# A third tile of each l fetched row by row, its DMAs issued from ScalarE in groups of eight

## The chip, the core and the metric

The kernel runs on one core of a Trainium2 chip. The metric is the device time of one execution in microseconds (us). The engines are named as in the profile: PE (TensorE), DVE (VectorE), ACT (ScalarE), POOL (GpSimd) and SP (SyncE). An l is one of the 200 positions of the history, and a step is one eighth of an l.

## The reference

A recommendation model scores 16384 users (B). Each has 200 items of history (L). For every l and user a row of 64 floats is looked up in a table of items, and an attention net of 36 hidden units weighs it:

```python
u = u_emb[user]; it = i_emb[item]; c = c_emb[cate]
h = i_emb[hist]                                   # L x B x 64
itb = broadcast(it, h.shape)
feat = concatenate([h, itb, h - itb, h * itb], axis=-1)
a = dice(feat @ au_W1 + au_b1, au_alpha, axis=1)  # statistics over B, for each l
w = a @ au_W2 + au_b2
cur = sum(w * h, axis=0)                          # over l
z = concatenate([u, it, c, cur], axis=-1)
z = dice(z @ W1 + b1, alpha1, axis=0)
z = dice(z @ W2 + b2, alpha2, axis=0)
return z @ W3 + b3
```

`dice(x)` normalises x by its mean and variance along the axis, takes a sigmoid p of that, and returns x * (p + alpha * (1 - p)). The lookup `i_emb[hist]` is 3,276,800 rows of 256 bytes.

## The kernel before, in words

The 16384 users of one l are 128 tiles (NT) of 128 users, one user a partition. Sixteen tiles (TD) make a chunk c, eight chunks (ND) an l, and the kernel takes one chunk a step: step k belongs to l = k // 8 and c = k % 8. A loop (L406, turned four times) holds 45 l each, written out; the last 20 l and the head come after it.

There are two ways in which a tile's rows get into the chip's memory.

- By gather: `fetch` (L270) issues one indirect DMA per tile on POOL (L117). It takes 128 row numbers from a column of `idx` and brings 128 rows. All tiles but two of each l come so: 126.
- By address: the last tile of the chunks c = 3 and c = 7 (`SIDES`, L26) is fetched row by row on SP. `rows_by_address` (L254) loads sixteen addresses from `addr` into registers at once (L258, TENSOR_LOAD) and issues sixteen DMAs of one row each (L265: a MOVE and a DMA). They land in one of three `side` tiles. In the turn of that chunk ACT copies the side tile into the chunk's rows (L301). `ask` (L356) spreads this over SP: half an l, four steps, for a tile.

The chunk's rows lie in one of five row buffers (`ROWS`). Step k, in the program's order:

1. `fetch(k)`: POOL issues the chunk's gathers, 16, or 15 where a side tile belongs to the chunk.
2. `gate(k - 10)` on ACT (L278, L279), `weights(k - 10)`: a product on DVE (L282) and a matmul into `wb`.
3. `hidden(k - 2)`: ACT brings the hidden layer from `px` (L290); `measure(k - 2)`: DVE takes its statistics (L295).
4. `turn(k - 1)`: the copy of the side tile (L301, two chunks of eight), four transposes on DVE (L146) into hT, matmuls on hT and on the item's rows, and a copy of hT into `ph` on ACT (L304).
5. `weigh(k - 10)` on DVE (L286, L287) adds to the sum over l; `product(k - 1)`: DVE (L307) and a last matmul into `px`.
6. Once per l, `moments`: small DVE operations and a square root on ACT (L160).

Each engine works through its own instructions in that order, which is written out by hand (`tc.manual_schedule`); semaphores put in by the framework hold an engine where it needs another's result. A DMA that SP issues by the framework waits for the DMA eight before it, since eight semaphores go round; so does a gather on POOL.

Per l SP also loads the row numbers of the next l (c = 0, L130) and its addresses (c = 2, L135), which DVE scales to bytes at c = 4 (L138). `column` (L87) says which column of `idx` a tile has.

Of the kernel before, what the change touches and what calls it, by code (L numbers as in the profile page):

```python
# [9 lines left out]
I32 = mybir.dt.int32  # L10
# [4 lines left out]
P = 128  # L15
D = 64
# [5 lines left out]
ROWS = 5  # L22
LAG = 10
XR = 9
IDX = 3
SIDES = (3, 7)  # L26
LOAD = 16
ROW = 4 * D
U8 = mybir.dt.uint8

# [2 lines left out]
def din_kernel(  # L33
# [24 lines left out]
    nc = tc.nc  # L58
    L, B = r_hist.shape
    NT = B // P  # L60
    TD = 2 * CD // P
    ND = NT // TD
    V = i_emb.shape[0]
# [2 lines left out]
    ZA = P // 2  # L66
    ZB = Z1 - ZA
    NS = len(SIDES)
    NC = NT - NS
    BODY = L - L % LPB if L > LPB else 0  # L70
    STATS = nc.vector.BN_STATS_DIM
# [5 lines left out]
    def make(name, *shape, dt=F32):  # L77
        return const.tile(list(shape), dt, name=name)

    def col(v):  # L80
        return v.rearrange("(p o) -> p o", o=1)
# [5 lines left out]
    def column(c, n):  # L87
        if c in SIDES and n == TD - 1:
            return NC + SIDES.index(c)
        return c * TD + n - sum(s < c for s in SIDES)  # L90

    def columns(v):
        return v[: NC * P].rearrange("(p n) -> p n", n=NC)

# [5 lines left out]
    rows = [make(f"rows{i}", P, TD, D) for i in range(ROWS)]  # L100
    hT = [make(f"hT{i}", P, CD) for i in range(LAG)]
    xs = [make(f"xs{i}", P, CD) for i in range(XR)]
    itT = [make(f"itT{c}", P, CD) for c in range(ND)]
    curT = [make(f"curT{c}", P, CD) for c in range(ND)]
    hm = make("hm", P, CD)
    y = make("y", P, CD)
    ucT = [make(f"ucT{i}", P, CD) for i in range(4)]
    idx = [make(f"idx{i}", P, NC, dt=I32) for i in range(IDX)]
    ids = [make(f"ids{i}", P, NT, dt=I32) for i in range(3)]
    side = [make(f"side{i}", P, D) for i in range(3)]  # L110
    addr = [make(f"addr{i}", 1, NS * P, dt=I32) for i in range(3)]
    stats = [make(f"st{i}", P, 2 * ND, STATS) for i in range(3)]
    rstds = [make(f"rs{i}", P, 1) for i in range(3)]
# [2 lines left out]
    def gather(dst, ids, n, table):  # L116
        nc.gpsimd.indirect_dma_start(  # L117
            out=dst[:, n, :],
            out_offset=None,
            in_=table,  # L120
            in_offset=bass.IndirectOffsetOnAxis(ap=ids, axis=0),
        )

    def load_ids(t, v):
        nc.sync.dma_start(t[:, :NC], columns(v))
        for s in range(NS):
            nc.sync.dma_start(t[:, NC + s : NC + s + 1], col(v[(NC + s) * P : (NC + s + 1) * P]))

    def load_hist_ids(i, l):
        nc.sync.dma_start(  # L130
            idx[i], r_hist[ds(l, 1), : NC * P].rearrange("l (p n) -> p (l n)", n=NC)
        )

    def load_addresses(i, l):
        nc.sync.dma_start(addr[i], r_hist[ds(l, 1), NC * P :])  # L135

    def scale_addresses(i):
        nc.vector.tensor_scalar_mul(addr[i], addr[i], ROW)  # L138

# [3 lines left out]
    def transpose(dst, of):  # L143
        for i in range(2):
            for e in range(2):
                nc.vector.transpose(by_tile(dst[ts(e, D)], i), of[ts(i, D), :, ts(e, S)])  # L146

    def layer(dst, pairs, first=True, last=True):
        for i in range(2):
            for j, (lhsT, rhs) in enumerate(pairs):  # L150
                nc.tensor.matmul(  # L151
                    dst[:, ts(i, CH)], lhsT, rhs[:, ts(i, CH)],
                    start=(first and j == 0), stop=(last and j == len(pairs) - 1),
                    skip_group_check=not (first and last),
                )
# [59 lines left out]
    al1a, al1b, al12 = make("al1a", P, 1), make("al1b", P, 1), make("al12", P, 1)  # L215
    same_a = make("same_a", P, P)
    same_b = make("same_b", P, P)
    lanes = make("lanes", P, P, dt=I32)
    lane = make("lane", P, P, dt=I32)

    def head_weights():
        for t in (w1a, w1b, w2a, w2b, w3, bias2, al2):
# [28 lines left out]

    flat = i_emb.rearrange("v d -> (v d)").bitcast(U8)

    def rows_by_address(m, l, part, n):  # L254
        s, dst = m % NS, side[m % 3].bitcast(U8)
        for b in range(0, n, LOAD):
            p0 = part * n + b
            _, at = nc.values_load_multi_w_load_instructions(  # L258
                addr[l % 3][:, s * P + p0 : s * P + p0 + LOAD],
                engines=(mybir.EngineType.SP,), min_val=0, max_val=ROW * (V - 1),  # L260
                skip_runtime_bounds_check_because="the DMA checks the address against the table",
            )
            for j, a in enumerate(at):
                p = p0 + j
                nc.sync.dma_start(dst[p : p + 1], flat[ds(a, ROW)].rearrange("(o d) -> o d", o=1))  # L265

    def has_side(k):
        return k % ND in SIDES

    def fetch(k):  # L270
        l, c = divmod(k, ND)
        for n in range(TD - has_side(k)):
            j = column(c, n)
            gather(rows[k % ROWS], idx[l % IDX][:, j : j + 1], n, i_emb)

    def gate(k):
        i = k // ND % 3
        nc.scalar.activation(pg, xs[k % XR], AF.Sigmoid, bias=shifts[i], scale=rstds[i])  # L278
        nc.scalar.activation(pg, pg, AF.Identity, bias=au_al, scale=au_1al)  # L279

    def weights(k):
        nc.vector.tensor_mul(y, pg, xs[k % XR])  # L282
        layer(wb, [(blk_w, y)])

    def weigh(k):
        nc.vector.scalar_tensor_tensor(wb, wb, au_bias2, hT[k % LAG], ALU.add, ALU.mult)  # L286
        nc.vector.tensor_add(curT[k % ND], wb, curT[k % ND])  # L287

    def hidden(k):
        nc.scalar.activation(xs[k % XR], px, AF.Identity, bias=au_bias)  # L290

    def measure(k):
        l, c = divmod(k, ND)
        for i in range(2):
            nc.vector.bn_stats(stats[l % 3][:, 2 * c + i, :], xs[k % XR][:, ts(i, CH)])  # L295

    def turn(k):
        if has_side(k):
            l, c = divmod(k, ND)
            m = l * NS + SIDES.index(c)  # L300
            nc.scalar.copy(rows[k % ROWS][:, TD - 1], side[m % 3])  # L301
        transpose(hT[k % LAG], rows[k % ROWS])
        layer(px, [(blk_h, hT[k % LAG]), (blk_i, itT[k % ND])], last=False)
        nc.scalar.copy(ph, hT[k % LAG])  # L304

    def product(k):
        nc.vector.tensor_mul(hm, ph, itT[k % ND])  # L307
        layer(px, [(blk_m, hm)], first=False)
# [21 lines left out]
    def step(k, last=None):  # L330

        def has(j):
            return last is None or j <= last

        if has(k):
            fetch(k)
        if has(k - LAG):
            gate(k - LAG)
            weights(k - LAG)
        if has(k - 2):  # L340
            hidden(k - 2)
            measure(k - 2)
        if has(k - 1):
            turn(k - 1)
        if has(k - LAG):
            weigh(k - LAG)
        if has(k - 1):
            product(k - 1)
        if has(k - 2) and (k - 2) % ND == ND - 1:
            moments((k - 2) // ND)  # L350

    PER = ND // NS

    def ask(k, end):  # L356
        m, part = divmod(k + 1, PER)
        if m < end * NS:
            rows_by_address(m, m // NS, part, P // PER)

    def steps(l0, n, end):
        for k in range(n * ND):
# [10 lines left out]
    with tc.manual_schedule():  # L373
        load_ids(ids[0], r_item)
        load_hist_ids(0, 0)
        load_addresses(0, 0)
        load_ids(ids[1], r_cate)
        load_ids(ids[2], r_user)
        nc.gpsimd.iota(lanes, pattern=[[1, P]], base=P, channel_multiplier=-1)
        attention_weights()  # L380
        for t in (*hT, *xs, *side, hm):
            nc.vector.memset(t, 0.0)  # L382
        for t in curT:
            nc.vector.memset(t, 0.0)
        for i in range(3):
            nc.vector.memset(rstds[i], 0.0)
            nc.vector.memset(shifts[i], 0.0)  # L387
        nc.vector.bn_stats(stats[-1 % 3][:, 0, :], hm[:, :CH])
        for c in range(1, 2 * ND):
            nc.vector.tensor_copy(stats[-1 % 3][:, c, :], stats[-1 % 3][:, 0, :])  # L390
        scale_addresses(0)
        layer(px, [(blk_m, hm)])

        for c in range(ND + 1):
            if c < ND:
                for n in range(TD):
                    j = column(c, n)
                    gather(rows[c % ROWS], ids[0][:, j : j + 1], n, i_emb)
            if c:
                transpose(itT[c - 1], rows[(c - 1) % ROWS])  # L400
        nc.vector.memset(rows[-1 % ROWS], 0.0)
        ask(-1, L)
        head_weights()

# [35 lines left out]
    with tc.manual_schedule():  # L440
# [54 lines left out]
        for c in range(ND):  # L495
# [13 lines left out]
            for q in range(4):  # L509
                c = 4 * g + q  # L510
                n, j = TD - (c in SIDES), column(c, 0)
                of = res[g][ts(q, S)]
# [4 lines left out]
                if c in SIDES:  # L517
                    j = column(c, TD - 1)
# [33 lines left out]
```

## Time and profile before

| | |
|---|---|
| median of three runs | 32128.78 us (32128.46 to 32131.62) |
| the profiled execution | 32101.94 us |
| its span, first to last instruction | 32100.2 us |
| granted clock of TensorE in it, mean | 0.719 |
| busy share of PE, DVE, ACT, POOL | 49%, 46%, 24%, 75% |
| gathers on POOL | 25200 of history, 128 each of items, users and categories |
| rows by address on SP | 51200 DMAs of 256 bytes |
| moved by the DMA engines | 881.57 MB, 27 GB/s over the span |

How to read it: "busy" counts what the engine itself executes. Register moves, semaphores, register loads (TENSOR_LOAD) and the issuing of a DMA are the sequencer's and are not in it, so SP has no busy time at all, and ACT's share would not grow by DMAs that it issues. Idle time in front of a group of instructions is put down to what ended it; "issue" means that nothing in the profile ended it. In a group's line stand the engine, the operation, out<-in, the count, then busy us and mean ns of one, then idle us and what ended most of it. In a line of a window stand its ends, its length, the busy time with the count, the granted clock, the DMA engines' busy share and GB/s. A line of the timeline has the start, the duration, the engine, the line and the operation, the count, and in brackets the idle time before it and who ended it.

### The profile page before, as it was taken

The page shows a single profiled execution, that of the slowest core. Times are in us where ns is not written, and L with a number is a line of the kernel's source. Part 1 is how long each engine was busy: PE and PEld are TensorE (multiplying, and loading weights), DVE is VectorE, ACT ScalarE, POOL GpSimd, SP SyncE. Part 2 cuts the span into 40 slices and gives each one's busy share as a digit, 9 for nine tenths or more (in the row PEclk, how much of TensorE's full clock was granted, in tenths as well). Part 3 has the DMA queues.
Part 4 walks back from the last instruction along what each step waited for, and adds up shares of the span by engine and source line. Part 5 has one row for each costly group of instructions (what it writes and reads, how often), then busy time and mean ns, then how long its engine had stood idle before and what let it go on. Part 6 is the DMA issues. An engine that isn't in the chain of part 4 may idle for free. (4 is left out here: it accounts for less than half of the span.)

```text
span 32100.2 us, 224464 instructions
## 1 busy us (share of the span) xinstructions
PE 15661.4 (49%) x26020; PEld 6253.8 (19%) x26020; DVE 14921.9 (46%) x18956; ACT 7823.3 (24%) x7481; POOL 24139.4 (75%) x25589
## 2 busy tenths in 40 slices
PE   4444444444444444444445444454444444445445
PEld 1111121111111111111112111121111211112111
DVE  4444444444444444444444444444444444444443
ACT  2222222222222222222222222222222222222222
POOL 7777777777777777777777777777777777777776
PEclk7777767776777777777777777777777777777777
DMA  1111111111111111111111111111111111111111
GB/s 28 28 28 28 28 28 28 28 27 28 28 28 28 28 28 28 28 27 28 28 28 28 28 28 28 28 28 28 28 28 28 28 28 28 28 28 28 28 28 22
DMA packets 958596, 881.57 MB, mean 27 GB/s; under 512 B 547488, under 2 KB 547688, under 8 KB 957032
## 3 DMA queue, kind: packets, MB, share of 16 engines
q0 software_dynamic: 818688, 839.97, 11.8%
q1 hardware_dynamic: 138056, 27.05, 0.4%
q14 instruction: 1352, 11.08, 0.1%
q8 instruction: 212, 3.47, 0.0%
q10 hardware_dynamic: 288, 0.00, 0.0%
HBM read 865.03 MB, written 0.13 MB: 27 GB/s over the span
## 5 line engine op out<-in xcount | busy, mean ns | idle before, releaser
L117 POOL DMA_INDIRECT rows<-in_L_rec_i_emb,idx x25200 | 23776.6, 944 | 7706.1 <-issue 7132.8
L151 PE MATMUL px<-hT,blk_h 128*128 128x512 f32 x6404 | 5661.5, 983 | 15033.9 <-DVE hT L146 15033.9
L146 DVE STREAM_TRANSPOSE hT<-rows 64x512 f32<-64x512 f32 x6404 | 4519.1, 706 | 12085.3 <-DMA rows<-in_L_rec_i_emb,idx 11421.6
L304 ACT COPY ph<-hT 128x1024 f32<-128x1024 f32 x1601 | 1627.1, 1016 | 18738.7 <-DVE hT L146 18738.7
L151 PEld LDWEIGHTS px<-hT,blk_h 128*128 128x128 f32 x6404 | 1816.6, 314 | 18047.2 <-issue 17233.6
L151 PE MATMUL px<-itT,blk_i 128*128 128x512 f32 x6404 | 4735.4, 832 | 0.0
L151 PE MATMUL wb<-y,blk_w 128*128 128x512 f32 x6440 | 3413.4, 657 | 1245.9 <-DVE y L282 1230.2
L295 DVE BATCH_NORM_STATS2 st<-xs 128x6 f32<-128x512 f32 x3204 | 2058.3, 684 | 3704.4 <-ACT xs L290 3704.4
L151 PE MATMUL px<-hm,blk_m 128*128 128x512 f32 x6408 | 3036.9, 596 | 38.1 <-DVE hm L382 36.4
L290 ACT ACTIVATE xs<-px,au_bias 128x1024 f32<-128x1024 f32 x1602 | 1781.6, 1112 | 4164.1 <-PE px L151 4164.1
L151 PEld LDWEIGHTS px<-itT,blk_i 128*128 128x128 f32 x6404 | 1862.1, 291 | 2859.9 <-issue 2859.9
L282 DVE TENSOR_TENSOR y<-pg,xs 128x1024 f32<-128x1024 f32 x1610 | 1954.9, 1214 | 736.6 <-ACT pg L279 736.4
L286 DVE SCALAR_TENSOR_TENSOR wb<-wb,au_bias,hT 128x1024 f32<-128x1024 f32 x1610 | 2081.1, 1293 | 82.2 <-PE wb L151 30.0
L287 DVE TENSOR_TENSOR curT<-wb,curT 128x1024 f32<-128x1024 f32 x1610 | 1971.2, 1224 | 54.8
L278 ACT ACTIVATE pg<-xs,sh,rs 128x1024 f32<-128x1024 f32 x1610 | 1937.3, 1203 | 79.9 <-DVE sh L387 42.7
L307 DVE TENSOR_TENSOR hm<-ph,itT 128x1024 f32<-128x1024 f32 x1601 | 1942.5, 1213 | 0.0
L279 ACT ACTIVATE pg<-pg,au_al,au_1al 128x1024 f32<-128x1024 f32 x1610 | 1895.1, 1177 | 54.1
L151 PEld LDWEIGHTS wb<-y,blk_w 128*128 128x128 f32 x6440 | 1307.8, 207 | 2976.1 <-issue 1538.0
L151 PEld LDWEIGHTS px<-hm,blk_m 128*128 128x128 f32 x6408 | 1195.9, 191 | 1686.8 <-issue 1236.5
L278 ACT ACT_TABLE_LOAD x206 | 264.3, 1283 | 77.5 <-PEq L406 57.4
L160 ACT ACT_TABLE_LOAD x203 | 260.4, 1283 | 7.5 <-PE pg L461 4.0
L160 ACT ACTIVATE std<-var,eps 128x1 f32<-128x1 f32 x201 | 59.2, 294 | 710.6 <-DVE var L327 710.6
(147 smaller groups left out, 1531.7 us busy)
## 6 DMA issues: line engine op xcount, KB each, us to landing
side<-in_L_rec_i_emb SPq DMA_DIRECT2D x51200, 0.2 KB
rows<-in_L_rec_i_emb,idx POOLq DMA_INDIRECT x25200, 2.4
idx<-in_r_hist SPq DMA_DIRECT2D x200, 63.0 KB
addr<-in_r_hist SPq DMA_DIRECT2D x200, 1.0 KB
rows<-in_L_rec_i_emb,ids POOLq DMA_INDIRECT x128, 2.4
rows<-in_L_rec_c_emb,ids POOLq DMA_INDIRECT x128, 2.3
rows<-in_L_rec_u_emb,ids POOLq DMA_INDIRECT x128, 2.4
w1a<-in_L_rec_W SPq DMA_DIRECT2D x4, 32.0 KB
```

The lines of the kernel that those rows point to most:

```text
L117: nc.gpsimd.indirect_dma_start(out=dst[:, n, :], out_offset=None, in_=table, in_offset=bass.IndirectOffsetOnAxis(ap=ids, axis=0),)
L146: nc.vector.transpose(by_tile(dst[ts(e, D)], i), of[ts(i, D), :, ts(e, S)])
L151: nc.tensor.matmul(dst[:, ts(i, CH)], lhsT, rhs[:, ts(i, CH)], start=(first and j == 0), stop=(last and j == len(pairs) - 1), skip_group_c ...
L278: nc.scalar.activation(pg, xs[k % XR], AF.Sigmoid, bias=shifts[i], scale=rstds[i])
L279: nc.scalar.activation(pg, pg, AF.Identity, bias=au_al, scale=au_1al)
L282: nc.vector.tensor_mul(y, pg, xs[k % XR])
L286: nc.vector.scalar_tensor_tensor(wb, wb, au_bias2, hT[k % LAG], ALU.add, ALU.mult)
L287: nc.vector.tensor_add(curT[k % ND], wb, curT[k % ND])
L290: nc.scalar.activation(xs[k % XR], px, AF.Identity, bias=au_bias)
L295: nc.vector.bn_stats(stats[l % 3][:, 2 * c + i, :], xs[k % XR][:, ts(i, CH)])
L304: nc.scalar.copy(ph, hT[k % LAG])
L307: nc.vector.tensor_mul(hm, ph, itT[k % ND])
```

## The change

A third tile of each l, the last one of the chunk c = 6, is fetched row by row, and its 128 DMAs are issued by ACT. `SIDES` has three chunks, so 125 tiles of an l are gathered (NC = 125); SP keeps c = 3 and c = 7 as they were.

ACT's share is cut into sixteen groups of eight rows: one TENSOR_LOAD of eight addresses and eight DMAs. `scalar_rows` deals them over the steps c = 0 to 6 of the same l: two groups a step, three in the steps of c = 3 and c = 6, none in that of c = 7. A step's groups go alternately into two places of its program: after `gate` and `weights` (slot 0), and after `measure` (slot 1). With three groups, two are in slot 0.

The rows land in one of three new tiles, `aside`. Each has a semaphore of its own, `landed`, that all 128 DMAs raise by 16; the framework's semaphores are not used for these DMAs, so none of them waits for an earlier one. In the turn of c = 6 (in step c = 7) ACT waits for 16 * 128 on the semaphore, clears it, and copies the tile into the chunk's rows.

Two constant tiles, `lanes` and `lane`, share memory with `ucT` now, the address tile has 384 words and not 256, and the lists of row numbers at the start come in one more DMA each. The diff, cut to its core:

```diff
-SIDES = (3, 7)
+BY_SP = (3, 7)
+BY_ACT = 6
+SIDES = (3, 6, 7)
 LOAD = 16
+GROUP = 8
...
+    NB = len(BY_SP)
     NC = NT - NS
...
+    aside = [make(f"aside{i}", P, D) for i in range(3)]
+    landed = [tc.alloc_semaphore(f"landed{i}") for i in range(3)]
     addr = [make(f"addr{i}", 1, NS * P, dt=I32) for i in range(3)]
...
-    lanes = make("lanes", P, P, dt=I32)
-    lane = make("lane", P, P, dt=I32)
+    lanes, lane = (ucT[i][:, :P].bitcast(I32) for i in range(2))
...
+    def addresses(l, s, p0, n, engine):
+        _, at = nc.values_load_multi_w_load_instructions(
+            addr[l % 3][:, s * P + p0 : s * P + p0 + n],
+            engines=(engine,), min_val=0, max_val=ROW * (V - 1),
...
+        )
+        return [flat[ds(a, ROW)].rearrange("(o d) -> o d", o=1) for a in at]
+
+    def rows_by_sync(m, part, n):
+        l, j = divmod(m, NB)
+        s, dst = SIDES.index(BY_SP[j]), side[m % 3].bitcast(U8)
+        for p0 in range(part * n, part * n + n, LOAD):
+            for j, row in enumerate(addresses(l, s, p0, LOAD, mybir.EngineType.SP)):
+                nc.sync.dma_start(dst[p0 + j : p0 + j + 1], row)
...
+    def rows_by_scalar(l, part):
+        s, dst = SIDES.index(BY_ACT), aside[l % 3].bitcast(U8)
+        key = open_group.setdefault(l, f"rows{next(groups)}")
+        for j, row in enumerate(addresses(l, s, part * GROUP, GROUP, mybir.EngineType.Activation)):
+            p = part * GROUP + j
+            dma = nc.scalar.dma_start(dst[p : p + 1], row).then_inc(landed[l % 3], 16)
+            tc.no_tile_sem_insts.add(dma.ins.name)
+            tc.add_to_no_dep_group(key, dma.ins)
+
+    def take_rows_by_scalar(l):
+        fence = nc.scalar.wait_ge(landed[l % 3], 16 * P)
+        tc.declare_fence(fence.ins, group=open_group.pop(l))
+        nc.scalar.sem_clear(landed[l % 3])
+        return aside[l % 3]
...
     def turn(k):
         if has_side(k):
             l, c = divmod(k, ND)
-            m = l * NS + SIDES.index(c)
-            nc.scalar.copy(rows[k % ROWS][:, TD - 1], side[m % 3])
+            if c == BY_ACT and l >= 0:
+                of = take_rows_by_scalar(l)
...
+            else:
+                of = side[(l * NB + BY_SP.index(c)) % 3]
+            nc.scalar.copy(rows[k % ROWS][:, TD - 1], of)
...
             gate(k - LAG)
             weights(k - LAG)
+        if has(k):
+            scalar_rows(k, 0)
         if has(k - 2):
             hidden(k - 2)
             measure(k - 2)
+        if has(k):
+            scalar_rows(k, 1)
         if has(k - 1):
             turn(k - 1)
...
+    def scalar_rows(k, slot):
+        l, c = divmod(k, ND)
+        if c > BY_ACT:
+            return
+        n = P // GROUP
+        mine = range(c * n // (BY_ACT + 1), (c + 1) * n // (BY_ACT + 1))
+        for part in mine[slot::2]:
+            rows_by_scalar(l, part)
```

More of the change, by code (lines that the diff above doesn't have):

```diff
@@ L252, in din_kernel @@
     flat = i_emb.rearrange("v d -> (v d)").bitcast(U8)
[L254 to L265, printed above, removed]
+    def addresses(l, s, p0, n, engine):
+        _, at = nc.values_load_multi_w_load_instructions(
+            addr[l % 3][:, s * P + p0 : s * P + p0 + n],
+            engines=(engine,), min_val=0, max_val=ROW * (V - 1),
+            skip_runtime_bounds_check_because="the DMA checks the address against the table",
+        )
[6 more added lines that the diff above has]
+                nc.sync.dma_start(dst[p0 + j : p0 + j + 1], row)
+    groups = iter(range(10**6))
+    open_group = {}
+    def rows_by_scalar(l, part):
[11 more added lines that the diff above has]
+        return aside[l % 3]
     def has_side(k):
@@ L299, in turn @@
             l, c = divmod(k, ND)
-            m = l * NS + SIDES.index(c)
-            nc.scalar.copy(rows[k % ROWS][:, TD - 1], side[m % 3])
+            if c == BY_ACT and l >= 0:
+                of = take_rows_by_scalar(l)
+            elif c == BY_ACT:
+                of = aside[l % 3]
+            else:
+                of = side[(l * NB + BY_SP.index(c)) % 3]
+            nc.scalar.copy(rows[k % ROWS][:, TD - 1], of)
         transpose(hT[k % LAG], rows[k % ROWS])
@@ L350, in step @@
             moments((k - 2) // ND)
-    PER = ND // NS
+    PER = ND // NB
     def ask(k, end):
         m, part = divmod(k + 1, PER)
-        if m < end * NS:
-            rows_by_address(m, m // NS, part, P // PER)
+        if m < end * NB:
+            rows_by_sync(m, part, P // PER)
+    def scalar_rows(k, slot):
[6 more added lines that the diff above has]
+            rows_by_scalar(l, part)
     def steps(l0, n, end):
@@ L380, in din_kernel @@
         attention_weights()
-        for t in (*hT, *xs, *side, hm):
+        for t in (*hT, *xs, *side, *aside, hm):
             nc.vector.memset(t, 0.0)
```

## The prediction

> **What bounds the kernel now.** I read first the page's busy times and slices, then the group of gathers (L117), then that line in four long windows, to get a rate from the trace and not from a mean.
>
> ```profile
> PE 15661.4 (49%) x26020; PEld 6253.8 (19%) x26020; DVE 14921.9 (46%) x18956; ACT 7823.3 (24%) x7481; POOL 24139.4 (75%) x25589
> ...
> POOL 7777777777777777777777777777777777777776
> ...
> DMA  1111111111111111111111111111111111111111
> ...
> q0 software_dynamic: 818688, 839.97, 11.8%
> q1 hardware_dynamic: 138056, 27.05, 0.4%
> ...
> L117 POOL DMA_INDIRECT rows<-in_L_rec_i_emb,idx x25200 | 23776.6, 944 | 7706.1 <-issue 7132.8
> ```
>
> No engine is above 75%, but POOL is level in all forty slices, and 7132.8 of its 7706.1 us of idle time end with "issue": nothing that the profile shows is waited for. 944 ns of work and a gap after it that belongs to the instruction make one gather. The windows (length, busy, count) give the sum of the two:
>
> ```profile
> 2000.00:6000.00 4000.00, 3023.06 (x3205) 0.72 0.12 28
> 10000.00:14000.00 4000.00, 3023.05 (x3205) 0.72 0.12 28
> ```
>
> 4000 us hold 3205 gathers (one of them cut by an edge), twice the same: 4000 / 3204 = 1.2484 us. The whole run is that rate: first gather at 2.9 us, last at 31963.8, 25584 of them (25200 of history, 3 x 128 others), so 25583 distances. Four of them are longer, where the loop of L406 turns or ends (8.94, 7.15, 7.15 and 4.04 us, 27.3 in all); the other 25579 take 31933.6 us, 1.2484 each. After the last gather's start the head needs 136.4 us. 2.9 + 31933.6 + 27.3 + 136.4 = 32100.2, the span. So POOL's count of gathers sets the time, and nothing else does between 2.9 and 31963.8 us. One l is 126 gathers, 157.3 us.
>
> Everybody else waits for it. ACT's longest wait (18738.7 us) is for the transposes (hT, L146), and these wait for gathers to land (11421.6 us).
>
> **What is removed.** One gather per l: 125 in place of 126. 200 x 1.2484 = 249.7 us of POOL's own path, with no cover to fill it: the next gather moves up. On the profiled execution: span 32100.2 - 249.7 = 31850.5; its own time is 1.7 us above its span (32101.94), so 31852.2. The median of the three runs is 32128.78, 26.8 above the profiled execution; I keep that distance and take 32128.78 - 249.7 = 31879.
>
> **What is added on ACT.** Per l sixteen groups: a TENSOR_LOAD of eight addresses, eight pairs of MOVE and DMA. 200 x 128 = 25600 DMAs, 3200 loads. ACT has issued only two DMAs so far; SP issues this very DMA 51200 times, so SP's rows are the nearest:
>
> ```profile
> 15032.13 11.53 SPq L265 DMA_DIRECT2D side<-in_L_rec_i_emb  x32
> ```
> ```profile
> L258 SPq TENSOR_LOAD <-addr x3200: 1130/1229/1483, 47.1 to 31498.1; - x189
> ```
> ```profile
> L519 ACTq DMA_DIRECT2D out<-res x2: 373/396/418, 32078.5 to 32092.8; - x2
> ```
>
> 32 DMAs with one load among them take 11.53 us from the first one's start to the last one's end. (11.53 - 0.23 for the last DMA - 1.29 for the load and the gap after it) / 31 = 0.323 us a DMA, MOVE included. A group is then 1.23 + 8 x 0.32 = 3.79 us. From below: eight registers, not sixteen, are loaded; the Trainium skill (DMA: Bandwidth & Descriptors, Latency and other measured facts) gives about 0.6 us as a floor of that load, so an estimate of 0.6 + 2.56 = 3.2. From above: the longest load, 1.48, and DMAs as long as ACT's own longest, 0.418 plus 0.1 for the MOVE: 1.48 + 8 x 0.52 = 5.6. I take 3.79, since form and count are SP's. ACT's work in one l is 38.7 us (the window 15000 to 15157.4); one more copy of a side tile (L301, 0.234) makes 38.9; 38.9 + 16 x 3.79 = 99.6 us of a new l of 156.05. With 5.6: 128.5. ACT becomes the bound at (156.05 - 38.9) / 16 = 7.3 us a group, 0.76 us a DMA.
>
> **Where in a step it stands.** Averages do not show order, so here is one step on ACT, and two instructions of DVE after it.
>
> ```profile
> 15007.01 1.02 ACT L304 COPY ph<-hT 128x1024 f32<-128x1024 f32 x1 [9.04 <-DVE hT L146]
> 15007.96 1.20 ACT L278 ACTIVATE pg<-xs,sh,rs 128x1024 f32<-128x1024 f32 x1
> 15009.20 1.18 ACT L279 ACTIVATE pg<-pg,au_al,au_1al 128x1024 f32<-128x1024 f32 x1
> 15012.77 1.11 ACT L290 ACTIVATE xs<-px,au_bias 128x1024 f32<-128x1024 f32 x1 [2.39 <-PE px L151]
> 15026.90 1.02 ACT L304 COPY ph<-hT 128x1024 f32<-128x1024 f32 x1 [13.02 <-DVE hT L146]
> ```
> ```profile
> 15013.91 1.28 DVE L295 BATCH_NORM_STATS2 st<-xs 128x6 f32<-128x512 f32 x2 [2.09 <-ACT xs L290]
> 15023.98 2.88 DVE L146 STREAM_TRANSPOSE hT<-rows 64x512 f32<-64x512 f32 x4 [8.78 <-DMA rows<-in_L_rec_i_emb,idx]
> ```
>
> The first groups of a step come after L279 (ends 15010.38) and before L290; the others after L290 and before the next L304. Queued behind the first is L290, and behind that DVE's statistics, which stand before the next transposes in DVE's order; behind the second are the copies of a turn. With one group each: L290 ends at 15010.38 + 3.79 + 1.11 = 15015.3, statistics at 15016.6, second group at 15019.1. The worst steps (c = 3 and 6) have two groups first and one after: L290 ends at 15019.1, statistics at 15020.4, the last group at 15022.9. The transposes cannot start before 15023.98, since their gathers have not landed, and L304 not before 15026.90: 3.6 and 4.0 us are left, and the whole addition is hidden by POOL. With 5.6 us a group L290 ends at 15022.7 and the statistics at 15024.0, just on the edge. If that cover is gone, a step runs late, and then five row buffers cover: POOL needs the buffer of step k again 4 steps (some 78 us) after its last gather, and DVE frees it 2.4 + 2.9 us after. POOL waits only for a delay of over 70 us that is not made good, and the steps with fewer groups, c = 7 with none, make it good.
>
> **The added wait.** In the turn of c = 6 ACT waits for 2048 on a landed semaphore. Behind it stand the copy into the rows, the transposes and L304. The last group was issued a step before (nearly 20 us); a gather lands 2.2 to 4.3 us after its issue. Cost 0; from above one landing, 4.3 us a step, inside the row buffers, so also 0 on the end. No gain is possible from it.
>
> **SP, DVE, POOL, start and end.** SP keeps its two tiles: per l 16 x 1.23 + 256 x 0.32 = 102 us plus two index loads; it now idles
>
> ```profile
> SPq L258 <- DVE y L282: 10009.2, 195, 77.5
> ```
>
> some 51 us per l, which covers the longer address load (384 words). If both issuers share one generator, ACT's 128 x 0.32 = 41 us are taken from that idle time: 106 + 41 = 147 of 156, still hidden. DVE gets three memsets of 0.11 us and a longer L138 (0.28 us, once per l). Does a gather slow down when more of these DMAs run beside it? SP's stream comes and goes, so the trace answers: distances of gathers with none of SP's DMAs in them average 1.2483 us (9586 of them), with four 1.2486 (8755). At that slope the new DMAs cost at most 0.0003 x 25384 = 8 us if each gather met four more; ACT issues for 16 x 3.79 = 61 of 156 us, so some 3; from below 0. The three more id loads at the start are SP's. Prologue, loop turns and head stay: 0, with a few us either way. Sum: -249.7 + 0 to 10.
>
> **A rule that speaks against it.** The row first: sixteen DMA engines are 12% busy and the gather has a fixed rate. The Trainium skill (DMA: Bandwidth & Descriptors, Issuing engines are not separate DMA queues) says that DMAs started by several engines run on the same sixteen DMA engines and that spreading them saves only issue time, usually small. By the rule alone the change would be worth about 0, 32129. By the row issue time is the whole path, and its share is 200 x 1.2484. I go by the row.
>
> **Rivals.**
> 1. POOL's path shortened as summed: 31879, with the unknowns 31865 to 31900. Chance 0.84.
> 2. ACT's groups cost 5 to 7 us (an issue on ACT next to activations is dearer than on SP), steps run late by turns, and POOL loses part: half the gain, 32004. Against it: the 70 us of row buffers. Chance 0.05 above 0.2%.
> 3. The work is moved but the end does not follow: another chain, of DVE or SP, is as long as POOL's. SP with a shared generator comes nearest, 147 of 156; at 157 the time would be 32129. Chance 0.04.
> 4. Slower: ACT pays each row's round trip before it issues the next. The skill gives 0.8 us as the least round trip to memory (same page and section as the load's floor). A group is 1.23 + 8 x 0.8 = 7.63, ACT's l 38.9 + 122.1 = 161.0 against 157.3 now: 200 x 3.7 = +740, 32870. It decides from 0.76 us a DMA (slower than before from 0.77). Against it: SP's 0.32 for the same DMA, and the new semaphores hold nothing back until the turn. No row shows 128 in flight on one semaphore. Chance 0.07.
>
> **Numbers.** About 0.2% (64 us) is what a measurement of this kernel can tell from no change. Faster is cases 1 and 2: 0.89; within 0.2%: 0.04; slower: 0.07. The range takes case 1 with its unknowns, a few us between executions, and the near part of case 2: 31862 to 31935.
>
> **What would show it.** Right: 25000 gathers of history, 1.2484 us apart in the same windows; span near 31850; ACT's wait for hT shorter, SP's wait still tens of us per l; DMAs of ACT 0.32 us apart. Wrong: longer idle time at L117 ended by ACT or DVE (cases 2, 4), gathers over 1.259 us apart (249.7 / 25000 = 0.010 us eats it all), or transposes that wait for ACT and not for gathers.

## The result and the profile after

| | before | changed |
|---|---|---|
| median of four runs | 32129.93 us | 31890.28 us (31864.21 to 31894.12) |
| ratio to before, 95% interval | | 0.9924, [0.9906, 0.9941] |
| the profiled execution, its span | 32101.94, 32100.2 us | 31864.21, 31862.4 us |

The kernel became 0.76% faster. The forecast was 31879 for the median and 31850.5 for the span of the profiled execution; both are 11 to 12 us short. The changed kernel's four runs include the profiled one, which is 26 to 30 us under the other three; the profiled execution of the kernel before, not among its four, is as far under those. Where that distance comes from was not traced (at the end).

The page of the changed kernel: busy times, the gathers (L123 now), the new queue of ACT's DMAs.

```profile
PE 15641.2 (49%) x26020; PEld 6235.8 (20%) x26020; DVE 14956.3 (47%) x18959; ACT 7911.4 (25%) x7681; POOL 23951.3 (75%) x25389
...
q10 hardware_dynamic: 51632, 6.66, 0.1%
...
L123 POOL DMA_INDIRECT rows<-in_L_rec_i_emb,idx x25000 | 23588.4, 944 | 7656.7 <-issue 7249.9
```

POOL has 200 gathers fewer, of the same 944 ns, and still idles for nothing that the profile can name. ACT's busy time grew by 88 us only, 47 of them the 200 new copies, since issuing is not counted. The same windows as before, for the gathers alone:

```profile
2000.00:6000.00 4000.00, 3022.83 (x3205) 0.72 0.13 28
10000.00:14000.00 4000.00, 3022.66 (x3205) 0.72 0.13 28
```

3205 again: POOL's pace did not change, there is less of it. What ACT's sequencer spends is seen in the lines that load and issue (minimum, median and maximum in ns), and one step on ACT shows where it went:

```profile
L260 ACTq TENSOR_LOAD <-addr x3200: 709/723/1039, 48.6 to 31363.9; - x189
```
```profile
L283 ACTq DMA_DIRECT2D aside<-in_L_rec_i_emb x25600: 217/218/595, 49.4 to 31367.2; - x199
```
```profile
15008.46 1.02 ACT L335 COPY ph<-hT 128x1024 f32<-128x1024 f32 x1 [8.20 <-DVE hT L152]
15009.41 1.20 ACT L304 ACTIVATE pg<-xs,sh,rs 128x1024 f32<-128x1024 f32 x1
15010.65 1.18 ACT L305 ACTIVATE pg<-pg,au_al,au_1al 128x1024 f32<-128x1024 f32 x1
15011.50 2.61 ACTq L283 DMA_DIRECT2D aside<-in_L_rec_i_emb  x8
15014.22 1.11 ACT L316 ACTIVATE xs<-px,au_bias 128x1024 f32<-128x1024 f32 x1 [2.39 <-PE px L157]
15015.09 2.65 ACTq L283 DMA_DIRECT2D aside<-in_L_rec_i_emb  x8
15028.39 1.02 ACT L335 COPY ph<-hT 128x1024 f32<-128x1024 f32 x1 [13.06 <-DVE hT L152]
```

ACT's sequencer loads the addresses and starts to issue while the activation before still runs: in the trace the load starts at 15010.65 with L305, the first group's DMAs start at 15011.50, and L305 ends at 15011.83. The group ends at 15014.11, where ACT would have waited for PE anyway: L316 starts 2.39 us after L305's end, as L290 did after L279's in the kernel before. From the load's start to the last DMA's end this group takes 3.46 us; over all 3200 groups the median is 3.53. A DMA with its MOVE takes 0.31, the first of a group 0.55.

### The profile page after: what moved, and what is told of

Its sections match the earlier page's. It is cut to its first block, busy times and chain, and to the rows that moved or that the text cites. A ratio compares the mean times of both kernels' runs of the same rounds, so it can differ in the third digit from the quotient of the medians.

```text
span 31862.4 us, 279674 instructions
## 1 busy us (share of the span) xinstructions
PE 15641.2 (49%) x26020; PEld 6235.8 (20%) x26020; DVE 14956.3 (47%) x18959; ACT 7911.4 (25%) x7681; POOL 23951.3 (75%) x25389
## 5 line engine op out<-in xcount | busy, mean ns | idle before, releaser
L123 POOL DMA_INDIRECT rows<-in_L_rec_i_emb,idx x25000 | 23588.4, 944 | 7656.7 <-issue 7249.9
L335 ACT COPY ph<-hT 128x1024 f32<-128x1024 f32 x1601 | 1627.3, 1016 | 15569.4 <-DVE hT L152 15560.5
L316 ACT ACTIVATE xs<-px,au_bias 128x1024 f32<-128x1024 f32 x1602 | 1783.5, 1113 | 5882.8 <-PE px L157 2957.5
L308 DVE TENSOR_TENSOR y<-pg,xs 128x1024 f32<-128x1024 f32 x1610 | 1954.1, 1214 | 745.0 <-ACT pg L305 744.8
L305 ACT ACTIVATE pg<-pg,au_al,au_1al 128x1024 f32<-128x1024 f32 x1610 | 1895.2, 1177 | 54.1
L332 ACT COPY rows<-side 128x64 f32<-128x64 f32 x401 | 97.9, 244 | 1237.6 <-DMA side<-in_L_rec_i_emb 1085.1
```

The source lines that it names most:

```text
L123: nc.gpsimd.indirect_dma_start(out=dst[:, n, :], out_offset=None, in_=table, in_offset=bass.IndirectOffsetOnAxis(ap=ids, axis=0),)
```

## The experiments

Each kernel was timed in three rounds beside the kernel before on the same chip. Ratios are to that.

**ACT's rows left out.**

```diff
-            if c == BY_ACT and l >= 0:
-                of = take_rows_by_scalar(l)
-            elif c == BY_ACT:
+            if c == BY_ACT:
                 of = aside[l % 3]
...
-        for part in mine[slot::2]:
-            rows_by_scalar(l, part)
+        return
```

> The changed kernel without ACT's 25600 row DMAs, its 3200 address loads and its waits on the landed semaphores; the tile of c = 6 stays zero, so its rows are left out of the computation. 125 gathers an l, as in the changed kernel. Theory (POOL's count of gathers alone sets the end, ACT's issuing is hidden): a profiled span of 31850 to 31865, the same as the changed kernel's 31862 within 10 us, and a timed ratio to before of 0.9924 within 0.001. Rival (issuing on ACT gives back part of the gain, or its DMAs slow the gathers): 20 us or more below the changed kernel, and distances of gathers shorter than 1.2484.

31860.63 us, ratio 0.9925 [0.9908, 0.9941]; span 31858.5. So the 25600 DMAs, loads and waits cost the changed kernel 3.9 us of span (31862.4 - 31858.5, one execution of each, on two chips). The gathers are 1.24844 us apart without the rows, 1.24857 with them: 0.00013 x 25379 = 3.3 of the 3.9 us. SP's largest wait (in total, times, the longest), without the rows and then with them:

```profile
SPq L260 <- DVE y L308: 9668.4, 195, 75.5
```
```profile
SPq L260 <- DVE y L308: 9610.0, 195, 75.3
```

ACT's DMAs took 58 us of SP's idle time in 200 l, 0.3 us an l. The 41 us an l that the prediction puts on a generator shared by both issuers did not come.

**The gather kept beside ACT's rows.**

```diff
+        if c == BY_ACT:
+            j = column(c, 0)
+            gather(rows[k % ROWS], idx[l % IDX][:, j : j + 1], TD - 1, i_emb)
```

> The changed kernel, and POOL gathers a sixteenth tile for c = 6 as well, into the place that ACT's copy overwrites afterwards: 126 gathers an l with all of ACT's DMAs beside them. Theory: a span of 31862 + 249.7 = 32112 within 12 us (the kernel before has 32100), so that the gain is the gather and nothing else. Rival (the rows by address cost POOL something themselves): over 32125, with gathers farther apart than 1.2490.

32105.50 us, ratio 1.0001 [0.9991, 1.0011]: with 126 gathers the whole gain is gone, all of ACT's work in place. Nine of the ten runs lie between 32104 and 32107, within the expectation. The tenth, the profiled execution, shows both signs of the rival, a span of 32136.1 and gathers 1.2499 us apart, 3201 of them in a window of 4000 us and not 3205:

```profile
2000.00:6000.00 4000.00, 3023.85 (x3201) 0.72 0.16 28
```

ACT's rows don't explain it, since the other nine have them too, and the changed kernel has them at 1.2486.

**Twice and four times the DMAs on ACT.**

```diff
+        spare = [t.bitcast(U8) for t in (*again, aside[(l + 1) % 3])]
...
-            dma = nc.scalar.dma_start(dst[p : p + 1], row).then_inc(landed[l % 3], 16)
...
+            for to in (dst, *spare[: TIMES - 1]):
+                dma = nc.scalar.dma_start(to[p : p + 1], row).then_inc(landed[l % 3], 16)
...
-    fence = nc.scalar.wait_ge(landed[l % 3], 16 * P)
+    fence = nc.scalar.wait_ge(landed[l % 3], 16 * P * TIMES)
```

> Each of ACT's row DMAs is issued twice, the second into a tile that nobody reads: 256 DMAs an l on ACT, groups of 0.72 + 16 x 0.31 and gaps, 5.8 us. By the prediction's sum ACT has 38.9 + 16 x 5.8 = 132 us of 156. Theory: hidden, span within 15 us of 31862. Rival (ACT's place in the order of a step decides, not its sum): the steps with three groups come to 8.7 + 2 x 5.8 = 20.3 us of 20.0, turns run late, 200 to 2000 us more.

31870.85 us, ratio 0.9928 [0.9911, 0.9944]: 10.2 us over the kernel without rows on the same chip, for twice the changed kernel's DMAs. Hidden, but not without a trace: the profiled execution alone, with a span of 31897.8 and gathers 1.2499 us apart, lies outside the expectation, and turns do run late. What the transposes wait for, in the changed kernel and then here:

```profile
DVE hT L152 <- DMA rows<-in_L_rec_i_emb,idx: 9110.0, 1419, 9.1
```
```profile
DVE hT L154 <- DMA rows<-in_L_rec_i_emb,idx: 4083.7, 786, 7.6
DVE hT L154 <- ACT rows L336: 766.5, 174, 5.4
```

They wait for gathers 786 times and not 1419, and 174 times for ACT's copy of a side tile. By the trace the transposes of the chunk c = 3 start 3.1 us after their last gather has landed (median; 11.3 at most), and 1.5 us in the changed kernel. POOL waits for DVE once, for 0.3 us: the row buffers take the delay up.

> Each of ACT's row DMAs is issued four times, three of them into tiles that nobody reads: groups of 0.72 + 32 x 0.31 and gaps, 10.8 us. Theory: ACT is the bound, past the 7.3 us a group of the prediction. An l takes 38.9 + 16 x 10.8 = 212 us if nothing of a group overlaps ACT's own work, 193 if its load and first DMAs run under the activation before it (1.2 us a group): a span between 39,000 and 43,000. Rival (POOL's five row buffers and the waits on landing are what limits, ACT's sequencer runs ahead): below 36,000.

44243.82 us, ratio 1.382 [1.3738, 1.3902]. ACT is the bound, past the range that was expected. What POOL waits for, and then what ACT waits for (in total, times, the longest):

```profile
POOL rows L125 <- DVE hT L154: 12262.3, 962, 17.6
```
```profile
ACT xs L320 <- issue: 18495.4, 1396, 22.4
ACT ph L339 <- issue: 10172.7, 1000, 11.4
ACT rows L336 <- issue: 2114.3, 204, 10.8
ACT rows L336 <- DMA side<-in_L_rec_i_emb: 2068.0, 195, 11.1
ACT ph L339 <- DVE hT L154: 1986.7, 601, 5.5
ACT xs L320 <- PE px L159: 510.6, 202, 2.8
ACT std L168 <- DVE var L362: 444.2, 201, 4.6
```

POOL waits for transposes now. ACT's idle time ended by "issue" is its own sequencer's issuing, and so is the row of the side tile, as long as a group. These four are 32850 us, 164.3 an l; the three real waits 2941, 14.7 an l; ACT's own work 7910, 39.6. Together 218.6 us an l, and the span less the 163 us ahead of the first gather of history and the 483 after the last one's start is 218.2 an l. The expectation, 212 without any overlap, left the waits out.

**All groups in one burst, with five and with three row buffers.**

```diff
-        mine = range(c * n // (BY_ACT + 1), (c + 1) * n // (BY_ACT + 1))
-        for part in mine[slot::2]:
-            rows_by_scalar(l, part)
+        if c == 0 and slot == 0:
+            for part in range(n):
+                rows_by_scalar(l, part)
```
```diff
-ROWS = 5
+ROWS = 3
```

> All sixteen groups of an l stand in one place, slot 0 of the step c = 0: a burst of 16 x 3.46 = 55 us on ACT, in front of the hidden layer's activation. Theory (five row buffers cover what ACT is late): the next transposes are 44 us late; POOL needs the buffer 73 us after it could have been freed, and the steps without groups, 11 us of work in 19.5, make the delay good within the l. Span as of the changed kernel, 31862 within 15 us. Rival (no such cover, a late step on ACT is paid): 44 us an l, 8800 us more.

31868.95 us, ratio 0.9927 [0.9911, 0.9944]; span 31867.1. DVE waits very long for ACT, and POOL does not wait for DVE by more than 0.3 us:

```profile
DVE st L321 <- ACT xs L316: 13961.1, 1401, 58.3
```
```profile
POOL rows L123 <- DVE hT L152: 25.3, 83, 0.3
```

> The burst of all sixteen groups in one step, with three row buffers in place of five. Theory: POOL needs a chunk's buffer again two steps (39 us) after its last gather and not four; the transposes that free it end 47 us after the time at which they would start in a step on time, so POOL waits about 10 us in every l: 200 x 10 = 2000 us more, 33,500 to 34,500. If the row buffers are not the cover (the theory falls): the same time as with five.

34462.60 us, ratio 1.0736 [1.0718, 1.0754]; span 34322.1. The same burst on ACT (128 DMAs from end to end), and what POOL waits for with three buffers:

```profile
15140.50 57.82 ACTq L283 DMA_DIRECT2D aside<-in_L_rec_i_emb  x128
```
```profile
POOL rows L123 <- DVE hT L152: 2402.7, 201, 26.3
```

12 us in each of 200 l, where the expectation's sum had 10. With five buffers the burst is as long (57.38 us in the l shown there); the buffers decide.

**ACT's DMAs on the framework's semaphores.**

```diff
-            dma = nc.scalar.dma_start(dst[p : p + 1], row).then_inc(landed[l % 3], 16)
-            tc.no_tile_sem_insts.add(dma.ins.name)
-            tc.add_to_no_dep_group(key, dma.ins)
+            nc.scalar.dma_start(dst[p : p + 1], row)
```

> ACT's row DMAs take the framework's eight semaphores, in turn with SP's, in place of semaphores of their own; the copy waits on the last eight. Each of these DMAs then waits for the landing of one that went before it, often of the other issuer's. Theory (the semaphores of its own are needed, since ACT and SP are coupled otherwise): SP cannot run ahead of ACT's place in its program, ACT stands in waits between activations, and POOL waits for turns that are late: slower than the kernel before, 33,000 to 38,000. Rival (SP's idle time and the row buffers cover that too): 31862 to 31900, the semaphores were not needed for the time.

31871.96 us, ratio 0.9928 [0.9912, 0.9945]. The theory of this run fell: the span of 31871.1 is 8.7 us above the changed kernel's, and 7.7 of them lie at the turns of the loop (43.7 us in place of 36.0). The coupling is there, and large:

```profile
SPq L271 <- DMA aside<-in_L_rec_i_emb: 9451.6, 4130, 100.4
```
```profile
ACT rows L325 <- DMA side<-in_L_rec_i_emb: 6285.1, 393, 20.6
ACT xs L309 <- PE px L156: 2486.5, 815, 3.8
ACT xs L309 <- DMA side<-in_L_rec_i_emb: 2420.0, 383, 7.9
```

SP waits 9451.6 us for landings of ACT's rows. In the changed kernel its 9610.0 us are one wait per l, at the first load of the next l's addresses, until DVE has scaled them; the view names the DVE instruction behind that one:

```profile
15071.92 0.34 DVE L144 TENSOR_SCALAR addr<-addr 1x384 int32<-1x384 int32 x1
15072.19 1.21 DVE L308 TENSOR_TENSOR y<-pg,xs 128x1024 f32<-128x1024 f32 x1
```

L144 ends at 15072.26, and in the trace SP's load starts at 15072.29, while L308 still runs. One wait took the other's place, in idle time that SP had. ACT's waits for SP's DMAs, 20.6 us at most, stay within the row buffers.

**A second tile on ACT.**

```diff
-BY_ACT = 6
-SIDES = (3, 6, 7)
+BY_ACT = (5, 6)
+SIDES = (3, 5, 6, 7)
...
-    aside = [make(f"aside{i}", P, D) for i in range(3)]
+    aside = [make(f"aside{i}", P, D) for i in range(2)]
...
-        n = P // GROUP
+        n = len(BY_ACT) * P // GROUP
```

> A fourth tile by address: ACT fetches the last tiles of c = 5 and c = 6, 32 groups of eight an l, in the steps c = 0 to 6; one landing tile and one semaphore for each. 124 gathers an l. Theory: 31862 - 249.7 = 31612, within 20 us, since ACT has 38.9 + 32 x 3.46 = 150 us of 154.8 without any overlap, and its loads run under the activations before them; ratio to before 0.9846. Rival (ACT is the bound already): an l of 155 us or more, so 31,700 and above.

32495.36 us, ratio 1.0139 [1.0113, 1.0165]: slower than both kernels with 124 gathers an l. Two steps on ACT:

```profile
15075.87 1.18 ACT L306 ACTIVATE pg<-pg,au_al,au_1al 128x1024 f32<-128x1024 f32 x1
15076.71 6.29 ACTq L284 DMA_DIRECT2D aside<-in_L_rec_i_emb  x16
15083.05 1.11 ACT L317 ACTIVATE xs<-px,au_bias 128x1024 f32<-128x1024 f32 x1 [6.00 <-issue]
15083.98 6.23 ACTq L284 DMA_DIRECT2D aside<-in_L_rec_i_emb  x16
15090.54 0.24 ACT L333 COPY rows<-side 128x64 f32<-128x64 f32 x1 [6.37 <-DMA side<-in_L_rec_i_emb]
15093.73 1.02 ACT L336 COPY ph<-hT 128x1024 f32<-128x1024 f32 x1 [2.95 <-DVE hT L152]
```

In these two steps ACT has no gap left but one: after the copy of a side tile it waits 2.95 us for transposes that waited for that copy, which stands behind the step's last groups. (The 6.37 us ahead of the copy are named as a wait for SP's DMA; they are ACT's own issuing in the line above.) An l takes 159.1 us on ACT, 150 in the sum that the expectation made. The other waits of this l are one at the square root and two in the step without groups:

```profile
15036.09 0.29 ACT L166 ACTIVATE std<-var,eps 128x1 f32<-128x1 f32 x1 [2.25 <-DVE var L359]
15144.97 1.11 ACT L317 ACTIVATE xs<-px,au_bias 128x1024 f32<-128x1024 f32 x1 [3.33 <-PE px L157]
15150.22 1.02 ACT L336 COPY ph<-hT 128x1024 f32<-128x1024 f32 x1 [4.00 <-DVE hT L152]
```

With 2.95 behind each of three copies that is 18.4 us of the 159.1. Work and issuing alone come to some 141, under POOL's 154.8; the sum left the waits out, and 8.9 us of them come from the copy's place behind the groups. By the trace the transposes start some 70 us after their last gather has landed, in every step (medians of 68 to 77 us), so the cover that the prediction gives to five row buffers, over 70 us, is used up. In the burst, where the worst step is 48 us late in the median, it was not.

**The copy ahead of slot 1, then groups of sixteen.**

```diff
+        if has(k - 1):
+            place(k - 1)
         if has(k):
             scalar_rows(k, 1)
```
```diff
-GROUP = 8
+GROUP = 16
```

> The kernel with two tiles by ACT, and the copy of a side tile stands before slot 1 and not after it, so that the transposes need not wait for a step's last groups on ACT. Theory (ACT's row of instructions is the bound there, 159 us an l, 2.95 us of it after each of three copies in which ACT waits for transposes that waited for it): 159 - 3 x 2.95 = 150 us, under POOL's 124 x 1.2484 = 154.8, so POOL is the bound again: a span of 31612 to 31650, ratio to before 0.985. Rival (the issuing alone fills ACT): above 32,000 still.

> The same with groups of sixteen: half the loads of addresses on ACT (1.23 us each in place of two of 0.72, about 3 us an l). Theory: if POOL is the bound already with groups of eight, the same time within 10 us; if ACT is, 3 us an l less, 600 us.

> The changed kernel, unaltered, beside the others on one chip. Theory: the kernel without ACT's rows has 31860.6 where the kernel before has 32102.5; this one 3 to 4 us more, 31864, from gathers that are 0.0001 us farther apart with the rows beside them. If issuing on ACT cost anything else, more than 10 us above.

These three ran on one occasion on which the kernel before itself took 47064.81 us, so none of the expectations could be tried. The copy ahead of slot 1 took 47087.45 us (ratio 1.0002 [0.9992, 1.0011]), with groups of sixteen 46317.20 (0.9834 [0.9817, 0.9850]), and the unaltered changed kernel 47756.84 (1.0138 [1.0121, 1.0155]). In the changed kernel's trace of that occasion a MOVE on SP, 29 ns elsewhere, takes up to 1480, and POOL waits for transposes:

```profile
L272 SPq MOVE side<-in_L_rec_i_emb x51200: 2/29/1480, 97.1 to 47311.9; - x200
```
```profile
POOL rows L123 <- DVE hT L152: 15532.6, 942, 46.3
```

In stretches, mostly of 3 to 30 us, each MOVE and DMA on SP and on ACT takes some 0.7 us, largely on both at once: of 17.3 ms of such stretches on ACT, 14.5 lie in those of SP. On that occasion the changed kernel loses 1.4% against the kernel before, and the kernel with two tiles and both edits, which moves twice as much, gains 1.7%. So the loss doesn't follow the amount that is moved. What makes the issuing slow stays open.

> Two tiles by ACT, the copy of a side tile before slot 1, groups of sixteen, once more on another occasion, since on the one before everything was 46% slower. ACT's row of an l: 159.9 in the kernel with two tiles, less 8.9 for three waits on transposes, less 3 for the loads, 148 us; POOL needs 124 x 1.2484 = 154.8. Theory: POOL is the bound, a span of 31612 to 31640, ratio to before 0.985, faster than both kernels. Rival (ACT's place in the steps still holds the transposes): 31,700 or more.

The kernel with both edits on another chip: 31620.40 us, ratio 0.9850 [0.9833, 0.9866], the fastest of all. POOL's gathers and its longest waits:

```profile
L123 POOL DMA_INDIRECT rows<-in_L_rec_i_emb,idx x24800 | 23408.3, 944 | 7593.4 <-issue 7245.8
```
```profile
POOL rows L123 <- issue: 7355.9, 24031, 9.3
POOL rows L123 <- DMA rows<-in_L_rec_i_emb,idx: 331.1, 1085, 0.3
```

No wait for transposes: POOL is the bound again, 400 gathers fewer than before, and that is 483 us. Which of the two edits it took is open, since the first alone ran only on the slow occasion. Groups of sixteen saved more than the 3 us an l that were expected: one takes 6.53 us in the median, two of eight in the kernel with two tiles 7.13, so sixteen of them save some 9.6 us an l. By these estimates either edit alone would have been enough: 159.1 - 8.9 = 150.2 and 159.1 - 9.6 = 149.5, both under 154.8.

## Why the prediction was right, point by point

- **POOL's count sets the end.** Shown from both sides: without ACT's rows the time stays (31860.63), with the gather back the gain goes (32105.50), and a second tile takes the next 240 us, once ACT no longer holds POOL up (31620.40).
- **The gather's 1.2484 us.** Held. The forecast was 249.7; from one profiled execution to the other the time fell by 237.7. The 12 us between are two terms that were set at nothing or nearly so. The distance grew by 0.00013 us, 3.3 us in all; the forecast had "some 3". The larger one is "Prologue, loop turns and head stay: 0": the four distances at the turns and the end of the loop sum to 36.0 us in place of 27.3. That is the step that was mis-sized, by 8.7 us. A middle turn, in the changed kernel and then in the one without ACT's rows:

```profile
14211.73 0.95 POOL L123 DMA_INDIRECT rows<-in_L_rec_i_emb,idx  x1 [0.30 <-issue]
14223.87 0.94 POOL L123 DMA_INDIRECT rows<-in_L_rec_i_emb,idx  x1 [11.19 <-issue]
```
```profile
14210.90 0.95 POOL L123 DMA_INDIRECT rows<-in_L_rec_i_emb,idx  x1 [0.30 <-issue]
14223.05 0.94 POOL L123 DMA_INDIRECT rows<-in_L_rec_i_emb,idx  x1 [11.19 <-issue]
```

  The same 11.19 us, so it is not ACT's issuing. With 126 gathers an l it is 6.2 us there, also with ACT's rows beside them (27.4 in all four). The middle turns go with the number of gathers in a round of the loop, and not in one direction: from gather to gather 7.15 us with 126 an l, 12.14 with 125, 8.46 with 124. In the trace a DRAIN on POOL at the turn is what ends later, 10.3 us after the last gather's start with 125 and 5.3 with 126. Why was not tried.
- **The median of 31879.** It rests on the 26.8 us between timed and profiled runs being there again. They were, on that chip (26 to 30 us); on three later ones the kernel before took 32102 to 32103 us. The prediction gives no reason for them, so that part is luck.
- **A group costs 3.79 us on ACT.** Mis-sized by less than a tenth, to the safe side: 3.53 in the median. The load of eight addresses is 0.72 us, near the 0.6 from which the prediction's lower bound starts, and it runs under the activation ahead of it, which the sum had left out. The upper bound of 5.6 was far off.
- **ACT is the bound at 7.3 us a group.** Bracketed only: 6.1 us a group (twice the DMAs, median) was hidden, 11.2 (four times) was not. And the sum alone is not the test: two tiles come to 7.1 us for each sixteenth of an l and were over, by waits that the sum leaves out.
- **Room in a step, and five row buffers behind it.** In the changed kernel the room was enough without the buffers: transposes start 1.4 to 1.6 us after their last gather has landed (medians by step), 0.2 to 1.5 in the kernel before. Twice the DMAs and the burst drew on the buffers, and with three POOL waited 12 us an l in the burst. ACT's wait for transposes became shorter, as forecast: 15560.5 us in place of 18738.7.
- **The added wait, and SP.** At 0, as forecast: in the trace ACT is never idle ahead of the 200 copies of the new tile. SP still idles 9610.0 us at that wait, against 10009.2.
- **The rivals.** The rule that speaks against the change says that issuing from another engine saves only issue time. That held, but its "usually small" did not: issue time was the path. Round trips paid one by one did not come: DMAs on ACT are 0.31 us apart. Semaphores of its own were not what kept that away; with the shared ones the span is 8.7 us longer.
- **Two small sums.** 38.9 + 16 x 3.79 is 99.5 and not 99.6, and 1.2484 + 0.010 is 1.2584 and not 1.259. Nothing rests on either.

## What to carry to other kernels

Where one engine issues at a fixed pace and waits for nothing, count its instructions and multiply by the distance measured in a long window: what moving one away gains is that distance, if the engine that takes the work has the time. Ask then not only for the sum on the engine that takes the work, but what stands behind the new instructions in its order, and how many buffers lie between that and the bound. Idle time ahead of an instruction can be the engine's own issuing, whatever the profile names as its end, and the instruction that a wait is put down to can be the one after the one that ended it.

## What the hardware showed that was not expected

- The gather's pace differs by execution. Away from POOL's waits it is 1.2484 to 1.2490 us in most profiled executions, 1.2499 in those of the kernel that keeps the gather and of the one with twice the DMAs, 32 and 29 us over their medians, and 1.2511 in that of the burst with three buffers. The timed runs of the kernel before on its first chip were 26.8 us over its profiled one, as a pace of some 1.2495 would make (an estimate), and these have no rows by ACT; that their gathers were slower was not seen.
- A sequencer runs ahead under its own engine's activation: a load of eight addresses (0.72 us, from 15010.65 on) and the first DMA of a group (from 15011.50 on) start before L305 ends at 15011.83.
- On one occasion all kernels took 46.3 to 47.8 ms, with SP's and ACT's MOVEs and DMAs at some 0.7 us each in stretches largely common to both.
